# Weighted sums of both halves of a block at its end, products two in the first half and one or none in the second, and two more buffers for the chunks of the mean

## The chip, the cores and the metric

The kernel runs on one core of a Trainium2 chip, in float32 throughout. A core has five engines that run their own queues in order: TensorE (PE; its weight loads are listed apart as PEld), VectorE (DVE), ScalarE (ACT), GpSimd (POOL) and SyncE (SP, which here only issues DMA). Matmul results go to eight banks of PSUM, 2 KB per partition each. The metric is the device time of one execution in microseconds (us), lower is better. The profile is of one execution.

## The reference

Two layers of a Perceiver: 256 query rows of 512 features (x) look at a context of 25088 rows (ctx). Each step adds its result to x after a layer norm.

```
x += x_norm @ W1.T + mean(ctx, rows) @ W2.T + b           # layer 0: the context only through its mean
x += banded self-attention, 16 heads of 32, window 128
x += mixture of 16 experts (4 chosen) + a shared one
Q = x_norm @ Wq + bq;  K = ctx @ Wk + bk;  V = ctx @ Wv + bv     # layer 1: cross-attention
scores[i, j, h] = Q[i, h] . K[j, h] / sqrt(32)
attn = softmax(scores, axis = i)                           # over the 256 queries, for each context row
x += (sum_j attn[i, j, h] V[j, h]) @ Wo + bo
x += windowed self-attention;  x += mixture of 8 experts (2 chosen), layer norm
```

The softmax runs over the queries, so each context row can be finished by itself: its maximum and its sum come from its own 256 scores per head.

## The kernel before

The context is cut into 49 chunks of 512 rows. Chunks 0 to 8 (NPRE) get their keys and values early, and these are stored to DRAM; the other 40 ("late" chunks) get them inside the cross-attention stage.

**Products.** Keys and values of a chunk are 512x512x512 matmuls done by a scheme with seven products of half-size matrices in place of eight (`seven`, line 392). One product is four matmuls of 128x128 by 128x256 (each shows as two records in the profile, so eight records at L401) into one PSUM bank, and is then added on VectorE to one quarter of the result (L423), or to two quarters in the case of one of the seven (S1). GpSimd makes the differences of the chunk that the scheme needs (L387) and one bias addition (L427). A chunk has 14 products.

**PSUM.** `ring` (line 62) is a queue of six banks: `take` gets the first, `give` puts one back at the end. Two more banks (`ac`) hold the sums of the attention. A taken bank is not checked for use; the framework makes its next writer wait for the last reader.

**The start.** From line 491 on: chunks 0 to 6 are loaded into tiles "ck" of the pool `early` (two buffers), and their products run on TensorE. Beside them all other chunks are loaded once for the mean (`load_sum`, L447), each into a tile "ct" of the pool `ctp` (three buffers), and summed by ScalarE (L443). SP issues all these loads in order, eight of the mean's to one ck. At the end `early` is closed; the weights of the first layer, l0x_w (2 MB, L530), the matmuls with them (L544, first with the normalised x, then with the mean), and the self-attention with its weights l0a_wqkv (L550) follow.

**The cross-attention stage** goes over 49 chunks of 4 sub-chunks of 128 context rows: 196 blocks. A block has two halves (`qp`), eight heads each. A half is:

- scores (L740): eight matmuls, four at a time in row groups of 32, into four banks (`scores`). Then for each bank r its maximum over the queries on VectorE (L749), and two exponentials on ScalarE (L754) with their sums. Banks 0 and 1 are given back inside `scores`, banks 2 and 3 after it.
- products of the next late chunk, drawn from the generator `stream` by `fill`. In the kernel before they are drawn in groups of 1, 2, 1, 2, 1 products (seven in five groups), about one group in each half, by a plan that has due times for each chunk. A group of one is drawn in front of bank 3's maximum (`between`), so that its addition stands ahead of that maximum in VectorE's queue; a group of two comes after the scores' work.
- weighted sums (`attend`, L767): eight matmuls, four at a time in column groups of 32. Their weights are the values divided by the sums (`scaled`, on GpSimd, L781, after a reciprocal on VectorE, L775), so a block's weighted sums come after the scores of the following block. The list `waiting` puts one half's weighted sums at the end of each half.

`queue <<` keeps instructions of the stage in the order in which they are written. Exponentials go to four buffers "e", one per half.

Of the kernel before, what the change touches and what calls it, by code (L numbers as in the profile page):

```python
# [9 lines left out]
F32 = mybir.dt.float32  # L10
# [5 lines left out]
P = 128  # L16
# [3 lines left out]
DC = D // P  # L20
# [3 lines left out]
JC = 512  # L24
SUB = JC // P
NPRE = 9
LN_EPS = 1e-5
SCALE = 1.0 / math.sqrt(HD)
# [4 lines left out]
C_L0A_BQ, C_L0A_BK, C_L1X_BQ, C_L1X_BK, C_L1A_BQ, C_L1A_BK = range(6)  # L33
# [4 lines left out]
def perceiver_kernel(  # L38
# [29 lines left out]
    def give(home):  # L68
        ring.append(home)

    def ps_mm(shape=None):
        tile, home = take("mm", shape)
        give(home)
        return tile
# [8 lines left out]
    ctp = ctp_scope.enter_context(tc.tile_pool(name="ctp", bufs=3, side="right"))  # L83
# [6 lines left out]
    early = early_scope.enter_context(tc.tile_pool(name="early", bufs=2, side="right"))  # L90
# [72 lines left out]
    def norm_T(roll=0, fill=None, untransposed=None):  # L163

        xT = work.tile([P, DC, NT], F32, tag="xT", name="xT", bufs=1)
        for t in range(T):
            mean, rs = norm_stats(x[:, t, :])
            xn = work.tile([P, D], F32, tag="xn", name="xn")
            nc.vector.tensor_scalar(xn, x[:, t, :], mean, rs, ALU.subtract, ALU.mult)
            if untransposed is not None:  # L170
                untransposed.append(xn)
            if t == 0 and fill:
                fill(2)
            tp = ps_mm([P, DC, P])
            for dc in range(DC):
                queue << nc.tensor.transpose(tp[:, dc, :], xn[:, dc * P : (dc + 1) * P], ident)
            at = (t * P - roll) % NT
            first = min(P, NT - at)
            nc.vector.tensor_copy(xT[:, :, at : at + first], tp[:, :, :first])
            if first < P:  # L180
                nc.vector.tensor_copy(xT[:, :, : P - first], tp[:, :, first:])
        return xT
# [7 lines left out]
    def feature_major(res, w, xT, col, scale=None):  # L190

        for fc in range(DC):
            ps = ps_mm([P, NT])
            for dc in range(DC):
                queue << nc.tensor.matmul(
                    ps, w[:, dc, fc * P : (fc + 1) * P], xT[:, dc, :],
                    start=dc == 0, stop=dc == DC - 1,
                )
            b = cols[:, col, fc : fc + 1]
            if scale is None:  # L200
                nc.vector.tensor_scalar(res[:, fc, :], ps, b, None, ALU.add)
            else:
                nc.vector.tensor_scalar(res[:, fc, :], ps, b, scale, ALU.add, ALU.mult)
# [239 lines left out]
            nc.scalar.activation(junk, ct[:, dc, :], AF.Identity, accum_out=csum[:, dc, c : c + 1])  # L443

    def load_sum(c):
        ct = ctp.tile([P, DC, JC], F32, tag="ct", name="ct")
        nc.sync.dma_start(out=ct, in_=ctx_d[c])  # L447
        chunk_sum(c, ct)

# [48 lines left out]
    for c in range(FIRST):  # L498
        units = early_chunk(c)
        n = min(8, len(rest)) if c + 1 < FIRST else len(rest)  # L500
# [115 lines left out]
    pending = None  # L616
    for e in range(NE0 + 1):
# [18 lines left out]
        pending = (e, hT, wt)  # L636
# [4 lines left out]
    with tc.tile_pool(name="xa", bufs=2) as xa:  # L641
        e_like = xa.tile([P, H // 2, NT], F32, tag="e", name="wq", bufs=4)
        wq = e_like.rearrange("p a b -> p (a b)").rearrange("p (c d) -> p c d", c=DC)
# [4 lines left out]
        late = list(range(NPRE, NCH))  # L648
        sequence, n = [], 0
# [58 lines left out]
                        yield step  # L708

        stream = projections()  # L710

        groups, done = (1, 2, 1, 2, 1), 0
        total = 2 * len(groups) * len(late)

        def fill(upto):
            nonlocal done
            while done < min(upto, total):
                for _ in range(groups[done % len(groups)]):
                    next(stream)
                done += 1  # L720

        fill(5)
        qT = xa.tile([P, DC, NT], F32, name="qT", bufs=1)
        feature_major(qT, wq, norm_T(fill=lambda n: fill(7)), C_L1X_BQ, SCALE)
        acc = [ps_ac([P, 2, NT]) for _ in range(2)]

        def restore(c):
# [7 lines left out]
        def scores(c, s, qp, e, nm, sm, between, finally_):  # L735
            sc, homes_of = zip(*(take("sc", [P, 2, NT]) for _ in range(4)))
            for i in range(2):
                for r in range(4):
                    part = slice(32 * r, 32 * r + 32)
                    queue << nc.tensor.matmul(  # L740
                        sc[r][:, i, :],
                        kTs[c][part, 2 * qp + i, s * P : (s + 1) * P],
                        qT[part, 2 * qp + i, :],
                        start=True, stop=True,
                    )
            for r in range(4):
                if r == 3:
                    between()
                queue << nc.vector.tensor_reduce(  # L749
                    nm[:, 2 * qp : 2 * qp + 2, r], sc[r], AX.X, ALU.max, negate=True  # L750
                )
                for i in range(2):
                    q = 2 * qp + i
                    queue << nc.scalar.activation(  # L754
                        e[:, 4 * i + r, :], sc[r][:, i, :], AF.Exp,
                        bias=nm[:, q, r : r + 1], accum_out=sm[:, q, r : r + 1],
                    )
                if r < 2:
                    give(homes_of[r])
            finally_()  # L760
            return homes_of[2:]

        def attend(first, last, qp, es, v):
            for i in range(2):
                for r in range(4):
                    h = 4 * (2 * qp + i) + r
                    queue << nc.tensor.matmul(  # L767
                        acc[qp][32 * r : 32 * r + 32, i, :],
                        v[:, h * HD : (h + 1) * HD], es[qp][:, 4 * i + r, :],
                        start=first and i == 0, stop=last, skip_group_check=True,  # L770
                    )
# [19 lines left out]
        due = [(0, done), (halves_of, total)]  # L791
        for at, c in enumerate(sequence):
            if c >= NPRE:
                k = 2 * len(groups) * (c - NPRE)
                due += [(2 * SUB * at, k + len(groups)), (2 * SUB * at + 2, k + 2 * len(groups))]
        plan, at = [done], due[0]
        while at[0] < halves_of:
            slope, to = max(((d[1] - at[1]) / (d[0] - at[0]), d) for d in due if d[0] > at[0])
            plan += [math.ceil(at[1] + slope * k) for k in range(1, to[0] - at[0] + 1)]
            at = to  # L800
        pending, n, waiting = None, 0, []
        restore(sequence[0])
        for c, following in zip(sequence, [*sequence[1:], None]):
            for s in range(SUB):
                if s == SUB - 1 and following is not None and following < NPRE:
                    restore(following)
                assert c < NPRE or ("k", c) in made
                nm = small.tile([P, Q, 4], F32, tag="nm", name="nm")
                sm = small.tile([P, Q, 4], F32, tag="sm", name="sm")
                es = []  # L810
                for qp in range(2):
                    e = xa.tile([P, H // 2, NT], F32, tag="e", name="e", bufs=4)
                    es.append(e)

                    def finally_():
                        if qp == 0 and pending is not None:
                            pc, ps, psm = pending[2]
                            pending[1][1] = scaled(pc, ps, inverse(psm))

                    def between():  # L820
                        if done < plan[n + 1] and groups[done % len(groups)] == 1:
                            fill(done + 1)

                    last = scores(c, s, qp, e, nm, sm, between, finally_)
                    n += 1
                    fill(min(plan[n], done + 1))
                    give(last[0])
                    fill(plan[n])
                    give(last[1])
                    assert qp == 0 or c < NPRE or ("v", c) in made  # L830

                    while waiting:
                        attend(*waiting.pop())
                    if pending is not None:
                        waiting.append((*pending[0], qp, *pending[1]))
                pending = ((n == 2, n == halves_of), [es, None], [c, s, sm])
            finished(c)
        pc, ps, psm = pending[2]
        pending[1][1] = scaled(pc, ps, inverse(psm))
        attend(*waiting.pop())  # L840
        for qp in range(2):
            attend(*pending[0], qp, *pending[1])

# [96 lines left out]
    upto = mini([P, NE1], "upto")  # L940
# [261 lines left out]
```

## Time and profile before

| | |
|---|---|
| median of 3 runs | 2849.3 us (2839.3 to 2852.96) |
| profiled execution | 2845.46 us, span 2843.7 us, mean granted TensorE clock 0.983 |
| TensorE busy | 2765.5 us (97%) |
| VectorE busy | 1727.7 us (61%) |
| ScalarE busy | 1712.9 us (60%) |
| stage of scores, 618 to 2467 us: TensorE, VectorE, ScalarE busy | 1849.7, 1412.6, 1470.7 us of 1851 |
| 8 to 165 us: TensorE busy, DMA share, rate | 146.3 of 157 us, 0.99, 393 GB/s |

The span is what lies between the first and the last instruction. A busy share is an average; matmuls are pipelined and the ends of their records are modelled, so durations of a group are best read from start to start. An entry in square brackets behind a row is the engine's idle time before it and what ended it.

### The profile page before, as it was taken

Reading aid. Unit: us, or ns where it says so; the run is one execution under the profiler, and the core shown is the slowest. Engines: PE = TensorE matmul, PEld = TensorE weight load, DVE = VectorE, ACT = ScalarE, POOL = GpSimd, SP = SyncE. Lnnn points to the kernel's source line nnn. Section 1 sums busy time; section 2 is a strip of 40 time slices with the busy share of each in tenths; the row PEclk is TensorE's granted clock in tenths of the full one; section 3 lists DMA queues with packets and bytes.
Section 4 is the critical chain, followed back from the end, with each engine's and each line's share of the span. In section 5 each row is a group of like instructions: output and inputs, shape, how many; then the busy total and the mean of one; then the engine's idle time right before and its main releaser. Section 6 shows DMA issues by size and latency. Waiting matters only on the chain. (4 is left out here: it accounts for less than half of the span.)

```text
span 2843.7 us, 56628 instructions
## 1 busy us (share of the span) xinstructions
PE 2765.5 (97%) x21236; PEld 1945.7 (68%) x21236; DVE 1727.7 (61%) x3065; ACT 1712.9 (60%) x7025; POOL 577.5 (20%) x532
## 2 busy tenths in 40 slices
PE   8998999999999999999999999999999999878998
PEld 7876777776666666666666666666666666556775
DVE  4345511147777777777777777777777777642101
ACT  6732100027778778778878878878888888621111
POOL 4221100012222323222222222222223222100000
PEclk9998999999999999999999999999999999978999
DMA  9971443410101010100101000101000101107774
GB/s 358 405 303 71 174 166 145 155 60 31 46 16 46 16 46 31 46 31 31 46 16 46 31 31 31 46 26 36 31 31 31 46 16 46 44 2 270 264 270 152
DMA packets 38099, 262.32 MB, mean 92 GB/s; under 512 B 4984, under 2 KB 8104, under 8 KB 10432
## 3 DMA queue, kind: packets, MB, share of 16 engines
q1 hardware_dynamic: 34640, 237.32, 22.2%
q0 software_dynamic: 3184, 21.33, 1.8%
q8 instruction: 173, 2.83, 0.4%
q14 instruction: 102, 0.84, 0.1%
HBM read 239.23 MB, written 19.40 MB: 91 GB/s over the span
## 5 line engine op out<-in xcount | busy, mean ns | idle before, releaser
L754 ACT ACTIVATE e<-ps_sc,nm 128x256 f32<-128x256 f32 x3136 | 1437.8, 484 | 376.7 <-DVE nm L749 376.4
L749 DVE TENSOR_REDUCE nm<-ps_sc 128x2 f32<-128x512 f32 x1568 | 994.6, 685 | 358.8 <-PE ps_sc L740 358.8
L754 ACT ACTIVATION_READ_ACCUMULATOR e<-ps_sc,nm 128x1 f32 x3136 | 676.9, 216 | 0.0
L767 PE MATMUL ps_ac<-e,vs 128*32 128x256 f32 x6272 | 421.6, 387 | 4.1 <-POOL vs L781 4.1
L401 PE MATMUL ps_kv<-ts,wq 128*128 128x256 f32 x1568 | 388.9, 392 | 9.1 <-DVE wq L365 6.5
L401 PE MATMUL ps_kv<-wq,ts 128*128 128x256 f32 x1568 | 386.8, 391 | 0.0
L781 POOL TENSOR_TENSOR vs<-v,rc 128x512 f32<-128x512 f32 x160 | 167.9, 1049 | 1015.7 <-DVE rc L775 1015.7
L401 PEld LDWEIGHTS ps_kv<-ts,wq 128*128 128x128 f32 x1568 | 287.0, 191 | 95.4 <-issue 26.7
L401 PEld LDWEIGHTS ps_kv<-wq,ts 128*128 128x128 f32 x1568 | 286.0, 190 | 84.7 <-issue 26.5
L740 PE MATMUL ps_sc<-qT,kT 32*128 32x256 f32 x4096 | 303.1, 401 | 1.3 <-ACT e L754 1.1
L767 PEld LDWEIGHTS ps_ac<-e,vs 128*32 128x32 f32 x6272 | 164.4, 109 | 202.6 <-issue 114.6
L423 DVE TENSOR_TENSOR v<-v,ps_kv 128x512 f32<-128x512 f32 x343 | 227.5, 676 | 102.1 <-PE ps_kv L401 57.6
L740 PEld LDWEIGHTS ps_sc<-qT,kT 32*128 32x128 f32 x4096 | 191.1, 184 | 116.0 <-ACT e L754 105.9
L401 PE MATMUL ps_kv<-wq,ct 128*128 128x256 f32 x1008 | 244.7, 386 | 0.0
L401 PE MATMUL ps_kv<-ct,wq 128*128 128x256 f32 x1008 | 242.4, 383 | 0.0
L423 DVE TENSOR_TENSOR kT<-kT,ps_kv 128x512 f32<-128x512 f32 x280 | 186.9, 680 | 64.6 <-PE ps_kv L401 54.2
L401 PEld LDWEIGHTS ps_kv<-wq,ct 128*128 128x128 f32 x1008 | 189.9, 192 | 38.3 <-ACT e L754 12.9
L401 PEld LDWEIGHTS ps_kv<-ct,wq 128*128 128x128 f32 x1008 | 188.1, 190 | 38.1 <-ACT e L754 12.6
L627 PE MATMUL ps_mm<-xT,we 128*128 128x256 f32 x816 | 178.8, 379 | 0.0
L627 PEld LDWEIGHTS ps_mm<-xT,we 128*128 128x128 f32 x816 | 155.0, 190 | 27.4 <-issue 7.2
L1091 ACT ACTIVATE hT<-ps_mm,b 128x128 f32<-128x128 f32 x128 | 36.6, 368 | 211.7 <-PE ps_mm L1085 158.2
L632 ACT ACTIVATE sg<-ps_mm 128x256 f32<-128x256 f32 x51 | 19.6, 385 | 229.4 <-PE ps_mm L627 229.4
(218 smaller groups left out, 2265.9 us busy)
## 6 DMA issues: line engine op xcount, KB each, us to landing
ct<-in_ctx_dram SPq DMA_DIRECT2D x84, 1024.0 KB, 6.4
we<-in_l1e_dram SPq DMA_DIRECT2D x64, 1024.0 KB, 6.8
we<-in_l0e_dram SPq DMA_DIRECT2D x17, 2304.0 KB, 8.6
kv<-kT POOLq DMA_DIRECT2D x9, 1024.0 KB, 9.9
kv<-v POOLq DMA_DIRECT2D x9, 1024.0 KB, 9.7
vp<-kv SPq DMA_DIRECT2D x9, 1024.0 KB, 5.0
kTp<-kv SPq DMA_DIRECT2D x8, 1024.0 KB, 4.8
ck<-in_ctx_dram SPq DMA_DIRECT2D x6, 1024.0 KB, 9.5
```

The source lines that it names most:

```text
L401: queue << nc.tensor.matmul(ps[:, m, :], fixed[:, d, m * P : (m + 1) * P], moving[:, d, :], start=d == 0, stop=d == 1,)
L423: queue << nc.vector.tensor_tensor(to, old, ps, ALU.subtract if a == W_A22 else ALU.add)
L627: queue << nc.tensor.matmul(gu[:, k, :], wk[:, dc, ic * P : (ic + 1) * P], xT[:, dc, :], start=dc == 0, stop=dc == DC - 1,)
L632: nc.scalar.activation(sg, gu[:, 0, :], AF.Silu)
L740: queue << nc.tensor.matmul(sc[r][:, i, :], kTs[c][part, 2 * qp + i, s * P : (s + 1) * P], qT[part, 2 * qp + i, :], start=True, stop=True,)
L749: queue << nc.vector.tensor_reduce(nm[:, 2 * qp : 2 * qp + 2, r], sc[r], AX.X, ALU.max, negate=True)
L754: queue << nc.scalar.activation(e[:, 4 * i + r, :], sc[r][:, i, :], AF.Exp, bias=nm[:, q, r : r + 1], accum_out=sm[:, q, r : r + 1],)
L767: queue << nc.tensor.matmul(acc[qp][32 * r : 32 * r + 32, i, :], v[:, h * HD : (h + 1) * HD], es[qp][:, 4 * i + r, :], start=first and i = ...
L781: queue << nc.gpsimd.tensor_mul(vs.rearrange("p (h d) -> p h d", h=H), vs_of[c, s].rearrange("p (h d) -> p h d", h=H), rc.unsqueeze(2).to_ ...
L1091: nc.scalar.activation(hT[:, fc, :], ps[:, fc, :], AF.Gelu, bias=b1[:, hf * FC + fc : hf * FC + fc + 1])
```

## The change

In the stage, the groups and the list `waiting` are gone. The plan is drawn up for whole blocks (`course`, in steps of two halves), and a block's products are split: up to two in the first half, the rest in the second. A product of the second half, if it is one, is drawn in front of bank 3's maximum (`between`); those of the first are drawn after the scores' work, one ahead of giving back bank 2 and one ahead of bank 3. The weighted sums of both halves of the block before are issued at the end of the second half. At the start, the mean's chunks go to two more buffers, tiles "cs" of the pool `early`, two chunks in five.

```diff
     def load_sum(c):
-        ct = ctp.tile([P, DC, JC], F32, tag="ct", name="ct")
+
+        if c % 5 in (1, 3):
+            ct = early.tile([P, DC, JC], F32, tag="cs", name="cs")
+        else:
+            ct = ctp.tile([P, DC, JC], F32, tag="ct", name="ct")
         nc.sync.dma_start(out=ct, in_=ctx_d[c])
         chunk_sum(c, ct)
...
-        groups, done = (1, 2, 1, 2, 1), 0
-        total = 2 * len(groups) * len(late)
+        total, done = 14 * len(late), 0
 
         def fill(upto):
             nonlocal done
             while done < min(upto, total):
-                for _ in range(groups[done % len(groups)]):
-                    next(stream)
+                next(stream)
                 done += 1
 
-        fill(5)
+        fill(7)
         qT = xa.tile([P, DC, NT], F32, name="qT", bufs=1)
-        feature_major(qT, wq, norm_T(fill=lambda n: fill(7)), C_L1X_BQ, SCALE)
+        feature_major(qT, wq, norm_T(fill=lambda n: fill(10)), C_L1X_BQ, SCALE)
...
             if c >= NPRE:
-                k = 2 * len(groups) * (c - NPRE)
-                due += [(2 * SUB * at, k + len(groups)), (2 * SUB * at + 2, k + 2 * len(groups))]
-        plan, at = [done], due[0]
+                k = 14 * (c - NPRE)
+                due += [(2 * SUB * at, k + 7), (2 * SUB * at + 2, k + 14)]
+        course, at = [done], due[0]
         while at[0] < halves_of:
             slope, to = max(((d[1] - at[1]) / (d[0] - at[0]), d) for d in due if d[0] > at[0])
-            plan += [math.ceil(at[1] + slope * k) for k in range(1, to[0] - at[0] + 1)]
+            course += [math.ceil(at[1] + slope * k) for k in range(2, to[0] - at[0] + 1, 2)]
             at = to
-        pending, n, waiting = None, 0, []
+        plan = []
+        for a, b in zip(course, course[1:]):
+            plan += [min(2, b - a), max(0, b - a - 2)]
+        pending, n = None, 0
...
                     def between():
-                        if done < plan[n + 1] and groups[done % len(groups)] == 1:
+                        if plan[n] == 1:
                             fill(done + 1)
 
+                    upto = done + plan[n]
                     last = scores(c, s, qp, e, nm, sm, between, finally_)
                     n += 1
-                    fill(min(plan[n], done + 1))
-                    give(last[0])
-                    fill(plan[n])
-                    give(last[1])
+                    for home in last:
+                        fill(min(upto, done + 1))
+                        give(home)
+                    fill(upto)
                     assert qp == 0 or c < NPRE or ("v", c) in made
 
-                    while waiting:
-                        attend(*waiting.pop())
-                    if pending is not None:
-                        waiting.append((*pending[0], qp, *pending[1]))
+                if pending is not None:
+                    for qp in range(2):
+                        attend(*pending[0], qp, *pending[1])
                 pending = ((n == 2, n == halves_of), [es, None], [c, s, sm])
             finished(c)
         pc, ps, psm = pending[2]
         pending[1][1] = scaled(pc, ps, inverse(psm))
-        attend(*waiting.pop())
         for qp in range(2):
             attend(*pending[0], qp, *pending[1])
```

## The prediction

> **What bounds the kernel now.** I read the table of busy times and the 40 slices first, then TensorE's waits, then its timeline inside the long cross-attention stage.
>
> ```profile
> span 2843.7 us, 56628 instructions
> PE 2765.5 (97%) x21236; PEld 1945.7 (68%) x21236; DVE 1727.7 (61%) x3065; ACT 1712.9 (60%) x7025; POOL 577.5 (20%) x532
> ...
> PE ps_sc L740 <- ACT e L754: 1.1, 5, 0.3
> ```
>
> TensorE (PE) is busy for 97%, and in the slices of the stage of scores (618 to 2467 us, 1846 us from its first scores to its last) for 90% or more throughout: here PE's own time counts. The last line, from TensorE's waits, says that scores waited for ScalarE's exponentials 1.1 us in all: a bank of PSUM was nearly always free in time. How near that is, the timeline shows (start, length, group of instructions):
>
> ```profile
> 1202.23 1.15 PE L740 MATMUL ps_sc<-qT,kT 32*128 32x256 f32 x16
> 1203.31 1.99 PE L401 MATMUL ps_kv<-ts,wq 128*128 128x256 f32 x8
> 1205.14 1.89 PE L401 MATMUL ps_kv<-ct,wq 128*128 128x256 f32 x8
> 1206.96 1.07 PE L767 MATMUL ps_ac<-e,vs 128*32 128x256 f32 x16
> 1207.96 1.15 PE L740 MATMUL ps_sc<-qT,kT 32*128 32x256 f32 x16
> 1209.03 1.99 PE L401 MATMUL ps_kv<-ts,wq 128*128 128x256 f32 x8
> 1210.96 1.07 PE L767 MATMUL ps_ac<-e,vs 128*32 128x256 f32 x16
> 1211.96 1.15 PE L740 MATMUL ps_sc<-qT,kT 32*128 32x256 f32 x16
> ```
>
> From start to start: scores (S) 1.07, one product (P) 1.93, two 3.65, weighted sums (A) 1.00. A half with one product takes 4.00 (1207.96 to 1211.96), one with two 5.73; two halves with three products 9.73, with two 8.00.
>
> The exponentials behind the scores of 1207.96 set when banks come free:
>
> ```profile
> 1209.91 0.47 ACT L754 ACTIVATE e<-ps_sc,nm 128x256 f32<-128x256 f32 x1 [1.97 <-DVE nm L749]
> ...
> 1211.63 0.21 ACT L754 ACTIVATION_READ_ACCUMULATOR e<-ps_sc,nm 128x1 f32 x1
> ```
>
> The first starts 1.95 after the scores (a maximum on VectorE lies between). Bank 1 of the scores (of 0 to 3) is read out at 1211.84, 3.88 after the scores began; bank 2 one pair of exponentials later (pairs start at 1209.91, 1210.82, 1211.72 in the same view), at 1212.75, 4.79 after. A half that lasts 4.00 and whose successor asks for bank 1 has 0.12 to spare.
>
> **The change, part by part.** *(1) Weighted sums of both halves at the block's end.* The built order of the changed kernel is S P P S P A A for a block of three products, S P P S A A for one of two. Working the plan out gives 164 blocks of three, 29 of two, and three empty ones at the end (where before also has six empty halves). The matmuls are the same; what goes is one group A between other groups. At the stage's end 32 records of A that follow each other last 1.93 where 16 last 1.07, so a second A costs 0.86, not 1.00. Three products: S P P 4.72, then S P A A 1.07+1.93+1.86 = 4.86, sum 9.58, or 0.15 under 9.73. Two: 4.72 + 1.07+1.86 = 7.65, or 0.35 under 8.00 (a switch into and out of products goes too). PE's own gain: 164 x 0.15 + 29 x 0.35 = 35 us.
>
> The Trainium skill agrees with the sign (TensorEngine Tiling (Array Packing), Key Properties: changing the tiling mode drains the engine), and by that rule alone the stage would end 35 us sooner. The same page speaks against it under PSUM Bottleneck: tiling speeds up the matmuls, not the emptying of PSUM, and the copy out can become the limit. It has no price; the rows above have one, and they decide, as follows.
>
> *(2) What the removed sums covered.* A ring of six banks serves S (four) and P (one each). Following the ring: after S P P the next scores ask for banks 0 and 1 of this half's scores, the first product's bank, and bank 2 of the scores. Bank 2 comes at 4.79 + 0.05 (the way of the semaphore, from restarts of PE at the stage's end); the fourth score matmul would start at 4.72 + 0.02. So 0.08 to 0.1 late, in about 140 blocks (after an empty second half the exponentials start earlier): 11 us. Before, the sums of 1.00 stood there.
>
> In the 29 blocks of two the second half is S A A, 2.93 of PE work, and the next scores ask last for its bank 1, free at 3.93. PE runs its queue in order, and behind that matmul stand the rest of the scores, the products and the sums of the half, so about 0.9 is lost each time: 26 us. Before shows this state at its end, six halves without a product (ScalarE's lines left out):
>
> ```profile
> 2457.37 1.32 PE L740 MATMUL ps_sc<-qT,kT 32*128 32x256 f32 x6
> 2458.91 1.12 PE L740 MATMUL ps_sc<-qT,kT 32*128 32x256 f32 x10 [0.22 <-ACT e L754]
> 2460.05 1.07 PE L767 MATMUL ps_ac<-e,vs 128*32 128x256 f32 x16
> 2461.06 1.29 PE L740 MATMUL ps_sc<-qT,kT 32*128 32x256 f32 x6
> ```
>
> The scores begin, stop after 6 of 16 records until ScalarE frees a bank, and the half takes 3.69 where PE needs 2.07.
>
> One product in seven is added twice on VectorE (0.60 each). As first product of a half its bank is free only at 3.57 (four maxima) + 0.24 (reciprocal) + 0.60 + 0.69 = 5.10 and the next scores want it at 4.74; as second product it is free at 6.2 and the second half's product, which now takes that same bank, wants it at 5.88. That is some 0.27 more in about 45 blocks: 12 us. In before such a half shows 4.04 for 4.00.
>
> Sum of the stage: -35 + 11 + 26 + 12 = +14. Bounds: -35 with no wait at all; +38 if each of the 140 waits is 0.25 and not 0.08. I take +14, whose largest term has a precedent in the trace.
>
> *(3) Two more buffers for the mean's chunks.* Between 20 and 190 us DMA moves 400 to 425 GB/s with the engines full, apart from 0.82 in 20 to 30 and 0.91 in 50 to 60: at most 2.7 us to win, and the order of bytes ahead of each chunk that PE waits for (2.2 us at 139.06, 2.7 at 168.30) is unchanged. I take -1.5 (0 to -2.7). SP and POOL issue the same transfers, SP's mean chunks up to two earlier.
>
> But the buffers lie in the pool that is closed just before the weights of the first layer are loaded, and in the built order that load (L530 before, L534 after) now carries waits on the seventh chunk's last use by PE, on ScalarE and on POOL; before it had none. It also slips behind three context loads on SP, and l0a_wqkv and the next context chunk stand behind it there.
>
> ```profile
> 166.22 0.42 SPq L530 DMA_DIRECT2D l0x_w<-in_l0x_w_dram  x1
> ```
>
> ```profile
> 192.97 1.89 PE L401 MATMUL ps_kv<-wq,ck 128*128 128x256 f32 x8
> ...
> 197.96 7.13 PE L544 MATMUL ps_mm<-l0x_w,xT 128*128 128x512 f32 x16 [0.51 <-DVE xT L179]
> ...
> 223.19 7.11 PE L195 MATMUL ps_mm<-xT,l0a_wqkv 128*128 128x256 f32 x24 [3.45 <-DMA l0a_wqkv<-in_l0a_wqkv_dram]
> ```
>
> The last product that reads ck is the one of 192.97, done at 194.9, so 2 MB can be asked for only then. 3 MB took 11.0 us on an idle queue (l0a_wqkv, issued at 212.04), 1 MB 5.0 (vp): 2 MB is 8.0. It lands at 202.9, the matmuls of 197.96 slip 5.0 us, and all behind them with it (l0a_wqkv, asked for after they end, slips as much, so its own wait stays). Bounds: 3.3 (6.4 us, the median of a context chunk) to 9 (12.2, its own time before). A gap of that length also costs clock: after the 3.45 us wait before 223.19 the granted clock was 0.63 and 0.52 until 227 (1.7 us lost), after the one before 168.30 it was 0.5 to 0.7 until 176 (3.3 lost). I take 2 more. Together +5.5.
>
> Sum against the profiled execution (2845.5 us, of which the span is 2843.7): +14 + 5.5 = +19.5, so 2865. The median of the runs is 3.8 above the profiled one: 2868; I write 2867.
>
> **The rivals.** *About the same, 2854 (chance 0.28).* The waits are half as dear: after a late bank VectorE's maxima come 0.4 sooner relative to the restart, so waits don't add, and the better-filled DMA pays for the late weights. For it: such restarts in the tail catch up. Against: in-order PE. Stage +5, start 0.
> *Faster, 2820 (chance 0.06).* Only PE's switches count, -35, with the start at +5.5. It decides once the three waits cost under 15 us instead of 49; the 3.88 of bank 1 against 2.93 makes that unlikely.
> *Much slower, 2896 (chance 0.14).* VectorE becomes late: two additions between the maxima of adjoining halves delay the exponentials, each first half waits 0.25 (stage +38), and the late weights cost their upper end (+9.5). Against: by the rows VectorE is done 1 us before the next half's first maximum.
> *No effect of the order* is excluded: the build shows it.
>
> **How the numbers follow.** The likeliest case has 0.52 and spans 2858 to 2878. The 80% range reaches into its neighbours: 2850 to 2885. About 0.5% (14 us) is what a measurement can tell from no change: faster below 2835, slower above 2863.5. Most of the likeliest case (0.48) and all of the worst one are slower, 0.62; the flat case and the rest are the same, 0.32; 0.06 faster.
>
> **What would show it.** In TensorE's timeline of the changed kernel: blocks of 9.6 to 9.7 with A as 32 records; waits of scores for exponentials of some tens of us in place of 1.1, most of it after halves S A A, with scores broken up as above; a wait of some 5 us for l0x_w near 198. The stage from first to last scores 1860 rather than 1846. Wrong if A A costs 2.00, if blocks of two take under 8.0, or if the load of l0x_w is not late.

## The result, and the profile after

The changed kernel takes 2866.4 us (median of 6 runs, 2863.64 to 2872.03); the kernel before, beside it, 2847.1 (6 runs, 2838.56 to 2852.96). The ratio is 1.0075, 95% interval 1.0053 to 1.0096: slower, by 19 us. The forecast was 2867. It is right in the sum, and the sum hides two errors that nearly cancel.

The page of the changed kernel, head and busy times:

```profile
span 2862.0 us, 56556 instructions
...
PE 2769.7 (97%) x21236; PEld 1994.4 (70%) x21236; DVE 1715.5 (60%) x3065; ACT 1717.1 (60%) x7025; POOL 577.0 (20%) x532
```

TensorE's waits in the stage of scores (line, what it waited for: us in all, times, longest):

```profile
PE ps_sc L741 <- ACT e L755: 8.6, 38, 1.4
PE ps_kv L401 <- DVE kT L423: 5.2, 17, 0.4
...
PE ps_kv L401 <- DVE v L423: 2.9, 9, 0.4
```

Scores waited 1.1 us for exponentials before, and products for VectorE's additions not at all. That names some 17 us, of which 14 lie ahead of the last six halves, where before has none. The timeline shows more (start, length, group; S is L741, P is L401, A is L768):

```profile
1213.85 1.25 PE L741 MATMUL ps_sc<-qT,kT 32*128 32x256 f32 x16
1215.03 1.99 PE L401 MATMUL ps_kv<-wq,ts 128*128 128x256 f32 x8
1216.95 1.93 PE L768 MATMUL ps_ac<-e,vs 128*32 128x256 f32 x32
1218.82 1.15 PE L741 MATMUL ps_sc<-qT,kT 32*128 32x256 f32 x16
1219.89 1.99 PE L401 MATMUL ps_kv<-wq,ct 128*128 128x256 f32 x8
1221.72 1.89 PE L401 MATMUL ps_kv<-wq,ts 128*128 128x256 f32 x8
1223.54 1.25 PE L741 MATMUL ps_sc<-qT,kT 32*128 32x256 f32 x16
```

The half S P P lasts 4.72 (1218.82 to 1223.54), as worked out, and 32 records of A 1.87. But the scores behind S P P start to start take 1.18 and not 1.07 (1213.85 to 1215.03): 0.11 of wait that no bracket shows; it lies inside the scores' record, which is 1.25 long and not 1.15. A block of three products takes 9.69 to 9.70. A block of two:

```profile
1098.63 1.25 PE L741 MATMUL ps_sc<-qT,kT 32*128 32x256 f32 x16
1099.81 1.93 PE L768 MATMUL ps_ac<-e,vs 128*32 128x256 f32 x32
1101.67 0.71 PE L741 MATMUL ps_sc<-qT,kT 32*128 32x256 f32 x6
1102.57 1.12 PE L741 MATMUL ps_sc<-qT,kT 32*128 32x256 f32 x10 [0.19 <-ACT e L755]
1103.62 1.99 PE L401 MATMUL ps_kv<-ct,wq 128*128 128x256 f32 x8
```

and ScalarE's exponentials for the scores of 1098.63 (the first of eight, and the end of the fourth):

```profile
1100.58 0.47 ACT L755 ACTIVATE e<-ps_sc,nm 128x256 f32<-128x256 f32 x1 [0.97 <-DVE nm L750]
...
1102.30 0.21 ACT L755 ACTIVATION_READ_ACCUMULATOR e<-ps_sc,nm 128x1 f32 x1
```

S A A is over after 3.04; bank 1 is read out at 1102.51, 3.88 after its scores began, and TensorE goes on at 1102.57. The scores take 1.95 from start to start (1101.67 to 1103.62), 0.88 more than their own 1.07; the bracket shows 0.19 of it.

From the first scores to the last record of the last sums the stage took 1857.7 us before (618.6 to 2476.3) and takes 1882.3 now (612.3 to 2494.6): 24.7 more. What follows it is equal. What precedes it is 6.4 shorter. TensorE's waits and DMA at the start, before:

```profile
139.06 1.97 PE L401 MATMUL ps_kv<-ck,wq 128*128 128x256 f32 x8 [2.19 <-DMA ck<-in_ctx_dram]
...
168.30 3.18 PE L401 MATMUL ps_kv<-ck,wq 128*128 128x256 f32 x8 [2.73 <-DMA ck<-in_ctx_dram]
```

and after (the first line is SP's issue of the weights of the first layer):

```profile
185.09 0.33 SPq L534 DMA_DIRECT2D l0x_w<-in_l0x_w_dram  x1
```

```profile
163.97 1.99 PE L401 MATMUL ps_kv<-ts,wq 128*128 128x256 f32 x8 [1.82 <-POOL ts L387]
...
192.74 8.72 PE L548 MATMUL ps_mm<-l0x_w,xT 128*128 128x512 f32 x16 [5.19 <-issue]
...
219.10 15.74 PE L195 MATMUL ps_mm<-xT,l0a_wqkv 128*128 128x256 f32 x64 [2.99 <-DMA l0a_wqkv<-in_l0a_wqkv_dram]
```

The two waits for ck are gone, and with the second the half clock behind it (TensorE reaches its last product of the start 9.9 us sooner than before). Then comes the wait for l0x_w, 5.19 where 5.0 was forecast, and its matmuls run slower, 8.72 for 7.13, at a granted clock of 0.57 from 192 to 196. The gain behind the matmuls with l0x_w is 3.6 (the next product starts at 208.17, before at 211.80), and 6.4 at the first scores; the 2.8 between them lie within what the start varies by itself (below), and their cause is open.

Stretches of the start, before (stretch, its length, busy us and counts of PE, PEld, DVE, ACT, POOL, granted clock, DMA share, GB/s):

```profile
20.00:60.00 40.00, 40.00 (x187) 35.22 (x186) 22.30 (x38) 30.12 (x97) 14.59 (x14) 1.00 0.93 373
60.00:100.00 40.00, 40.00 (x188) 35.20 (x187) 18.20 (x27) 30.92 (x99) 11.51 (x12) 1.00 1.01 403
100.00:130.00 30.00, 29.80 (x138) 25.93 (x137) 12.70 (x19) 22.47 (x73) 8.36 (x8) 1.00 1.01 399
```

and after:

```profile
20.00:60.00 40.00, 40.00 (x187) 35.22 (x186) 21.72 (x37) 33.20 (x107) 14.96 (x15) 1.00 1.01 422
60.00:100.00 40.00, 40.00 (x187) 35.22 (x186) 18.42 (x28) 32.73 (x104) 11.16 (x11) 1.00 1.01 423
100.00:130.00 30.00, 30.00 (x140) 26.41 (x139) 13.37 (x20) 22.93 (x73) 8.34 (x8) 1.00 1.01 423
```

A DMA share of 1.01 stands for 399 to 403 GB/s in the one and for 423 in the other. A full share was no ceiling.

### The profile page after: what moved, and what is told of

It reads as the page before. It is cut to its first block, busy times and chain, and to the rows that moved or that the text cites. A ratio compares the mean times of both kernels' runs of the same rounds, so it can differ in the third digit from the quotient of the medians.

```text
span 2862.0 us, 56556 instructions
## 1 busy us (share of the span) xinstructions
PE 2769.7 (97%) x21236; PEld 1994.4 (70%) x21236; DVE 1715.5 (60%) x3065; ACT 1717.1 (60%) x7025; POOL 577.0 (20%) x532
## 5 line engine op out<-in xcount | busy, mean ns | idle before, releaser
L768 PE MATMUL ps_ac<-e,vs 128*32 128x256 f32 x6272 | 381.9, 384 | 4.1 <-POOL vs L782 4.1
L401 PE MATMUL ps_kv<-ts,wq 128*128 128x256 f32 x1568 | 377.5, 387 | 4.9 <-POOL ts L387 4.9
L401 PE MATMUL ps_kv<-wq,ts 128*128 128x256 f32 x1568 | 378.0, 386 | 0.0
L401 PEld LDWEIGHTS ps_kv<-ts,wq 128*128 128x128 f32 x1568 | 290.9, 190 | 73.3 <-ACT e L755 12.9
L401 PEld LDWEIGHTS ps_kv<-wq,ts 128*128 128x128 f32 x1568 | 289.3, 190 | 69.4 <-DVE v L423 15.3
L741 PE MATMUL ps_sc<-qT,kT 32*128 32x256 f32 x4096 | 326.0, 402 | 6.0 <-ACT e L755 6.0
L768 PEld LDWEIGHTS ps_ac<-e,vs 128*32 128x32 f32 x6272 | 184.5, 110 | 172.2 <-issue 57.1
L741 PEld LDWEIGHTS ps_sc<-qT,kT 32*128 32x128 f32 x4096 | 209.1, 184 | 115.0 <-ACT e L755 67.4
L401 PE MATMUL ps_kv<-ct,wq 128*128 128x256 f32 x1008 | 246.9, 388 | 5.8 <-DVE kT L423 5.2
L401 PE MATMUL ps_kv<-wq,ct 128*128 128x256 f32 x1008 | 247.3, 388 | 2.9 <-DVE v L423 2.9
L401 PEld LDWEIGHTS ps_kv<-ct,wq 128*128 128x128 f32 x1008 | 184.1, 190 | 58.4 <-PE ps_sc L741 12.9
L401 PEld LDWEIGHTS ps_kv<-wq,ct 128*128 128x128 f32 x1008 | 186.4, 191 | 51.0 <-issue 8.0
L741 PE MATMUL ps_sc<-qT,kTp 32*128 32x256 f32 x2176 | 172.9, 402 | 2.6 <-ACT e L755 2.6
```

Source lines behind the costliest of these rows:

```text
L401: queue << nc.tensor.matmul(ps[:, m, :], fixed[:, d, m * P : (m + 1) * P], moving[:, d, :], start=d == 0, stop=d == 1,)
L741: queue << nc.tensor.matmul(sc[r][:, i, :], kTs[c][part, 2 * qp + i, s * P : (s + 1) * P], qT[part, 2 * qp + i, :], start=True, stop=True,)
L768: queue << nc.tensor.matmul(acc[qp][32 * r : 32 * r + 32, i, :], v[:, h * HD : (h + 1) * HD], es[qp][:, 4 * i + r, :], start=first and i = ...
```

## The experiments

First all of them in one table. "First scores" and "stage" (to the last record of the last sums) are from each kernel's profiled execution. The start varies by itself: seven kernels with before's start, itself among them, have their first scores between 617.0 and 621.6. A row without a ratio is a single run, beside 2844.7 for the kernel before (*unsummed* beside 2846.6).

| kernel | us | ratio, 95% interval | first scores | stage |
|---|---|---|---|---|
| before | 2846.6 | | 618.6 | 1857.7 |
| changed | 2866.4 | 1.0075, 1.0053 to 1.0096 | 612.3 | 1882.3 |
| order | 2872.5 | 1.0086, 1.0072 to 1.0099 | 619.7 | 1884.9 |
| buffers | 2841.5 | 0.9981, 0.9973 to 0.9989 | 615.0 | 1858.4 |
| buffers_free | 2836.4 | 0.9969, 0.9958 to 0.9980 | 607.2 | 1858.3 |
| held | 2858.7 | 1.0048, 1.0036 to 1.0060 | 617.0 | 1870.5 |
| before_nosum | 2842.4 | | 620.9 | 1854.6 |
| order_nosum | 2845.4 | | 619.0 | 1857.8 |
| order_oneuse | 2864.5 | | 619.3 | 1871.2 |
| one_one | 2886.1 | | 621.6 | 1895.0 |
| four_free | 2836.8 | 0.9962, 0.9949 to 0.9975 | 610.5 | 1858.3 |
| shared_sum | 2857.8 | 1.0040, 1.0025 to 1.0056 | 628.9 | 1858.2 |
| unsummed | 2837.3 | | 609.5 | 1857.5 |

### The two parts apart

*order*: the changed kernel without its new buffers.

```diff
     def load_sum(c):
-        if c % 5 in (1, 3):
-            ct = early.tile([P, DC, JC], F32, tag="cs", name="cs")
-        else:
-            ct = ctp.tile([P, DC, JC], F32, tag="ct", name="ct")
+        ct = ctp.tile([P, DC, JC], F32, tag="ct", name="ct")
```

> The changed order of the stage of scores alone, with before's three buffers for the mean's chunks. Theory: the stage loses 24.7 us in the changed kernel's trace (1873.3 against 1848.7 from the first scores to the start of the last sums) whatever happens before it, so the time is before + 25, about 2872, and the start (first scores near 618.6) is as before. Rival (the prediction's sums): stage +14, about 2861. Second rival: the stage is long because it begins after another start, then less than +10.

*buffers*: the kernel before with only that edit of `load_sum`, the other way round.

> The five buffers alone, with before's stage of scores. Theory: the start wins what the changed kernel's trace shows, first scores 6.4 us sooner, so about 2841; the load of l0x_w is asked for near 185 and TensorE waits some 5 us for it. Rival (the prediction's step: DMA was full already, so only the late weights count): first scores 5.5 us later, about 2853.

Measured: 2872.5 and 2841.5, as the theory has it; both forecasts of the prediction's sums (2861, 2853) are missed. The stage of *order* is 27.2 longer than before: all its halves but the last six together 22.8 (23.3 in the changed kernel), the last six, which have no product, 4.4 (1.4); that tail differs from kernel to kernel. The two parts add: +25.9 and -5.2 is +20.7, against +19.3 for the change. So the order costs, and the buffers win. The first scores of *buffers* come 3.6 us sooner, where 6.4 was expected. TensorE's timeline of *buffers* repeats that of the changed kernel, the wait for l0x_w with it:

```profile
192.80 8.62 PE L548 MATMUL ps_mm<-l0x_w,xT 128*128 128x512 f32 x16 [5.24 <-issue]
...
219.77 12.48 PE L195 MATMUL ps_mm<-xT,l0a_wqkv 128*128 128x256 f32 x49 [3.71 <-DMA l0a_wqkv<-in_l0a_wqkv_dram]
```

### What the order's loss consists of

All kernels of this part have before's three buffers.

*held*: no half without a product; a block of two has its products as 1 and 1, and one group of sums waits for its first half.

```diff
-            plan += [min(2, b - a), max(0, b - a - 2)]
+            plan += [(b - a + 1) // 2, (b - a) // 2]
...
                     fill(upto)
+                    while held:
+                        attend(*held.pop())
...
                 if pending is not None:
-                    for qp in range(2):
-                        attend(*pending[0], qp, *pending[1])
+                    attend(*pending[0], 0, *pending[1])
+                    held.append((*pending[0], 1, *pending[1]))
+                    if n == halves_of or sum(plan[n : n + 2]) > 2:
+                        attend(*held.pop())
```

> Three buffers; the sums of a block are held so that no half is without a product or short of sums: products 2 and 1, or 1 and 1 in a block of two; ahead of a block of two one group of sums waits for that block's first half. Orders S P P S P A | S P A S P A A for a pair of three and two, S P P S P A A elsewhere. Theory: the pair takes 8.73 + 8.97 = 17.70 and not 18.34 us (9.70 for three products, 4.73 + 3.04 + 0.87 of waiting for two), so 29 x 0.64 = 18.6 us of the order's 24.7 go, about 2853. Rival: the loss sits in the halves S P P and S P A A themselves, then the stage stays within 5 us of the changed order's, about 2870.

Measured: the stage is 14.4 shorter than in *order*, 12.8 over before and not 6; 2858.7 where 2853 was expected. The direction is the theory's, and the rival (nothing gained) falls. Most of the missing 7 us stands in its 59 halves S P A, 4.16 in the mean where 4.00 was expected: most of those behind S P P take 4.10 (the bank-2 wait of 0.1 is in them too), and 17 take 4.35 to 4.49.

*one_one*: the same even split, but with both sums at the block's end as in *order*.

```diff
-            plan += [min(2, b - a), max(0, b - a - 2)]
+            plan += [(b - a + 1) // 2, (b - a) // 2]
```

> The changed order (three buffers), but a block of two products has one in each half: S P S P A A in place of S P P S A A; no half is without a product. Theory: what counts is that a half must not end before 3.93 us, when bank 1 is read out. S P of 3.00 is as short as S A A of 2.93, so the wait of 0.9 only moves: the two halves take 3.00 + 0.93 + 4.97 = 8.9, and the stage is some 5 us longer than the changed order's 1884.9. Rival: a half without a product is what costs (one more switch in a row, no cover for VectorE), then the 29 x 0.87 = 25 us go, and the stage is about 1860.

Measured: stage 10.1 longer than in *order*. Expected was 5, the rival -25. A half without a product is not what costs; a half that is too short is (TensorE's timeline of *one_one*; in the kernels without the new buffers S is L737 and A L764):

```profile
1105.15 1.15 PE L737 MATMUL ps_sc<-qT,kT 32*128 32x256 f32 x16
1106.22 1.99 PE L401 MATMUL ps_kv<-ct,wq 128*128 128x256 f32 x8
1108.15 0.72 PE L737 MATMUL ps_sc<-qT,kT 32*128 32x256 f32 x4
1109.08 1.13 PE L737 MATMUL ps_sc<-qT,kT 32*128 32x256 f32 x12 [0.22 <-ACT e L751]
```

S P is done after 3.00, the next scores stop at once, and go on at 1109.08, 3.93 after the scores of 1105.15 began: within 0.01 of the 3.94 of the empty half (1098.63 to 1102.57). The two halves take 8.84 in the mean (3.00 + 5.84), against 8.65 for S P P, S A A and the wait behind it: 29 x 0.19 = 5.5. The rest of the 10.1 lies in other halves and in the tail.

*before_nosum* and *order_nosum*: the exponentials of the stage without their sums, so that banks of scores come free sooner.

```diff
-                        bias=nm[:, q, r : r + 1], accum_out=sm[:, q, r : r + 1],
+                        bias=nm[:, q, r : r + 1],
...
-                sm = small.tile([P, Q, 4], F32, tag="sm", name="sm")
...
+        sm = xa.tile([P, Q, 4], F32, name="sm1", bufs=1)
+        nc.vector.memset(sm, 1.0)
```

> The kernel before with the exponentials in the stage of scores not summed (the sums of the weights are left out, a tile of ones stands in for them), so that ScalarE hands the banks of scores back sooner. Theory: before, banks are in time already, so the stage (first scores to the end of the last sums, 1857.7 us) stays within 3 us, and halves stay 5.73 and 4.00; only the last empty halves shorten.

> The changed order (three buffers) with the same sums left out. Theory: TensorE waits in it for banks that ScalarE holds; without them the order shows its own worth on TensorE, 35 us less than before, of which the products added twice still cost some 13: stage 20 to 35 us under that of the kernel before with the sums left out, S P P 4.72, S P A A 4.86 (5.2 where a product is added twice), S A A 2.93 with no wait of 0.87 after it. Rival: the loss lies on TensorE itself (switches, the later sums): the stage is still some 25 us over.

Measured: in the kernel before the last six halves get 6.4 us shorter and all others 3.4 longer (the 42 halves behind a product added twice go from 4.04 to 4.11), together 3.0 us. *order* gives 27.1, 19.3 of it ahead of the last six halves. The order's loss shrinks from 27.2 to 3.2, ahead of the last six halves from 22.8 to 0.2: it hangs on how long exponentials hold the banks. That it does not turn into a gain of 20 misses the expectation, and the halves tell why. S P P is 4.73 and S P A A 4.86, TensorE's own times: the bank-2 wait is gone. But the half behind S A A is still 5.34 (5.60 with the sums), as TensorE's timeline of *order_nosum* shows:

```profile
1101.71 1.93 PE L764 MATMUL ps_ac<-e,vs 128*32 128x256 f32 x32
1103.57 1.76 PE L737 MATMUL ps_sc<-qT,kT 32*128 32x256 f32 x16
1105.26 1.99 PE L401 MATMUL ps_kv<-ct,wq 128*128 128x256 f32 x8
```

ScalarE's view of it:

```profile
1102.58 3.03 ACT L751 ACTIVATE e<-ps_sc,nm 128x256 f32<-128x256 f32 x8 [1.63 <-DVE nm L746]
```

An exponential without its sum still takes 3.03 / 8 = 0.38 (0.45 with it), and the first starts 1.95 after the scores as before, so bank 1 comes at 1.95 + 4 x 0.38 = 3.47, half a microsecond behind the end of S A A. And 44 halves with a product added twice take 5.3, since VectorE's additions are not touched. 28 x 0.61 + 44 x 0.43 = 36 us of waits stand against what TensorE gains, and the two nearly cancel. In *order* the waits are 57 us, so leaving the sums out took away about 20 and not all.

*order_oneuse*: the second addition left out.

```diff
-            (W_S1, ts[:, 0], ((c22, c21), (c12, c12))),
+            (W_S1, ts[:, 0], ((c22, c21),)),
```

> The changed order (three buffers), with the second addition of the product that is added twice left out (so one quarter of keys and values lacks a term). Theory: 45 halves wait 0.24 to 0.33 for that product's bank, so the stage is some 13 us shorter than with it (1884.9 to about 1872), and S P A A of 5.2 and 5.3 become 4.86 to 4.97. Rival: those halves are long for another reason (the block's place, the bank of the scores), then the stage stays within 3 us.

Measured: stage 13.7 shorter (1871.2), and the halves S P A A of 5.2 to 5.3 become 4.86 to 4.97, all but two. The 28 waits of TensorE for VectorE's kT, v and kTp in the changed kernel (17 + 9 + 2) fit the halves of 5.30 that follow a product added twice as second of its half. TensorE's timeline of the changed kernel shows one:

```profile
1039.88 1.15 PE L741 MATMUL ps_sc<-qT,kTp 32*128 32x256 f32 x16
1041.42 1.97 PE L401 MATMUL ps_kv<-wq,ct 128*128 128x256 f32 x8 [0.39 <-DVE v L423]
1043.31 1.93 PE L768 MATMUL ps_ac<-e,vs 128*32 128x256 f32 x32
```

### Why more buffers help

*buffers_free*: the kernel before with two more buffers that do not stand in the way of l0x_w.

```diff
     early_scope = ExitStack()
+    cs_scope = ExitStack()
     early = early_scope.enter_context(tc.tile_pool(name="early", bufs=2, side="right"))
+    csp = cs_scope.enter_context(tc.tile_pool(name="csp", bufs=2, side="right"))
...
     def load_sum(c):
-        ct = ctp.tile([P, DC, JC], F32, tag="ct", name="ct")
+        if c % 5 in (1, 3) and c < 40:
+            ct = csp.tile([P, DC, JC], F32, tag="cs", name="cs")
+        else:
+            ct = ctp.tile([P, DC, JC], F32, tag="ct", name="ct")
...
+    cs_scope.close()
     early_scope.close()
```

> Five buffers with before's stage, but the two new ones lie at the free end of the memory and only chunks below 40 use them, so that the load of l0x_w waits for nothing. Theory: the buffers' whole gain stays: 6.4 us as in the changed kernel, plus the 5.2 us wait and the 1.6 to 3.6 us of slower clock after it: first scores 13 us sooner than before, about 2834. Rival: the 2 MB of l0x_w, asked for some 20 us sooner, take the DMA from the chunks that TensorE waits for, and the waits for ck and ts come back: first scores only 4 to 7 us sooner, about 2841.

Measured: 2836.4, ratio 0.9969 (0.9958 to 0.9980), faster than both kernels. The load of l0x_w is asked for at 158.22 and its matmuls wait 0.55 (5.24 in *buffers*); they take 7.11 again and not 8.62. First scores 11.4 us sooner than before (13 was expected, 4 to 7 by the rival). So the late load cost what the prediction said, and what the buffers win ahead of it is about 10 us, not 1.5.

*four_free*: the same with one more buffer and not two (`c % 4 == 1`, `bufs=1`).

> One more buffer for the mean's chunks and not two (every fourth chunk below 40, at the free end of the memory, the load of l0x_w waits for nothing), before's stage. Theory: three buffers leave DMA too little in flight while ScalarE sums a chunk; a fourth covers most of it: 415 to 422 GB/s between 20 and 130 us, first scores 9 to 12 us sooner than before, about 2836. Rival: the rate grows by equal steps with each buffer: 408 GB/s, first scores 5 to 6 us sooner, about 2841.

Measured: 2836.8; 412, 421 and 422 GB/s in the three stretches, first scores 8.1 us sooner (9 to 12 expected, 5 to 6 by the rival). One buffer does nearly all.

*unsummed*: three buffers, but chunks from the eighth on are loaded and not summed (the mean is taken over the first seven).

```diff
     def chunk_sum(c, ct):
...
-        for dc in range(DC):
-            junk = ...
+        if c < FIRST:
+            for dc in range(DC):
+                junk = ...
```

> Three buffers, before's stage; the mean's chunks are loaded but not summed (the mean is taken over the first seven chunks alone), so a buffer is free as soon as it has landed. Theory (a buffer is held for the 2.45 us of ScalarE's sums): 420 GB/s and more between 20 and 130 us with three buffers, first scores 9 to 12 us sooner. Rival (the number of loads in flight alone): within 5 of before's 400 GB/s, first scores as before.

Measured, in the same stretches:

```profile
20.00:60.00 40.00, 40.00 (x187) 35.20 (x187) 21.90 (x37) 5.60 (x18) 14.64 (x14) 1.00 1.01 409
60.00:100.00 40.00, 40.00 (x187) 35.22 (x186) 18.21 (x27) 2.56 (x8) 11.39 (x12) 1.00 1.01 414
100.00:130.00 30.00, 30.00 (x141) 26.41 (x140) 13.36 (x20) 2.56 (x8) 8.32 (x8) 1.00 1.01 420
```

Three buffers do it too, if nothing holds them after they have landed; first scores at 609.5, 9.1 sooner. The rate falls a little short of the expected 420 at first, but the rival (the number of buffers alone) falls. Nor is it ScalarE's reading of the chunks that slows the loads: *four_free* keeps all of it and has 421 to 422.

*shared_sum*: three buffers, two of the four sums of each chunk on VectorE.

```diff
         for dc in range(DC):
+            if c >= FIRST and dc >= 2:
+                nc.vector.tensor_reduce(csum[:, dc, c : c + 1], ct[:, dc, :], AX.X, ALU.add)
+                continue
```

> Three buffers, before's stage, but of the four sums of each of the mean's chunks two are taken by VectorE, so that a buffer is held some 1.2 us after its landing and not 2.45. Theory: the rate is set by how long a buffer is held; it rises from 400 to 410 to 422 GB/s, and with it the waits for ck go, first scores 6 to 11 us sooner, about 2839. Rival: only the number of loads in flight counts: 400 GB/s as before, about 2847. What could spoil it: VectorE takes its queue in order, and a sum that waits for its chunk holds the additions that TensorE's banks wait for.

Measured: 2857.8, slower, by what the expectation named as its spoiler. VectorE, by its waits between 20 and 160 us, stood still for chunks that had not landed,

```profile
DVE csum L443 <- DMA ct<-in_ctx_dram: 42.9, 17, 6.9
```

TensorE waited 15 us for its additions, and the loads ran at 381 to 385 GB/s. It says nothing on how long a buffer may be held.

## Why the prediction was right, and where it was not

**The time.** 2867 against 2866.4, but stage +14 and start +5.5 were in truth +24.7 and -6.4. The sum, 18.3, agrees with 19.5 by luck. (2865 and 3.8 are 2868.8 and not 2868; that changes nothing.)

**(1) TensorE's own gain: right.** 35 us were forecast. All halves but the last six take 1852.0 us in the changed kernel; less the 57 us of waits below they come to 1795, against 1828.7 before: 34. A A takes 1.86 to 1.87 and S P P 4.73, as worked out. No kernel had all waits removed, so the 34 are worked out, from the measured sums and from TensorE's own times for each kind of half.

**(2) The waits: the right three, sized too small.** Against TensorE's own 4.73, 4.86 and 2.93:

| wait | forecast | measured |
|---|---|---|
| scores behind S P P, for bank 2 | 0.08 x 140 = 11 | 0.11 in most: 15 in S P A A, 3 in S A A |
| scores behind S A A, for bank 1 | 0.9 x 29 = 26 | 0.88 x 28 = 25 |
| the product added twice | 0.27 x 45 = 12 | 14 (*order_oneuse*) |
| sum | 49 | 57 |

The step that failed in size is "0.08 to 0.1 late, in about 140 blocks": it is about 0.11, and the S A A halves have it too. With 34 for 35, and 1.4 from the tail, that is the way from +14 to +24.7. The bank-1 time of 3.88, read from one half of the kernel before, is the same to the hundredth in the half of the changed kernel shown above, and it set the 3.93 of *one_one*. The flat rival, by which the waits are half as dear and do not add, is out: the waits came to 57 us and not to half of 49, and the double addition, forecast at 12, gave back 13.7 when it was left out. The reading of the Trainium skill's PSUM Bottleneck (TensorEngine Tiling (Array Packing)), that emptying PSUM can become the limit, was the one to follow: about 20 of the 57 us of waits went with the sums of the exponentials.

**(3) The start: wrong in sign.** The step that failed: "Between 20 and 190 us DMA moves 400 to 425 GB/s with the engines full", so "at most 2.7 us to win" and "I take -1.5". The share was taken for a limit. Before's own profile spoke against both readings, in the view of stretches of 10 us:

```profile
100.00:110.00 10.00, 10.00 (x48) 8.81 (x47) 2.75 (x4) 7.62 (x27) 0.00 (x0) 1.00 1.01 425
110.00:120.00 10.00, 9.80 (x46) 8.32 (x45) 5.52 (x9) 9.98 (x33) 8.36 (x8) 1.00 1.01 355
...
140.00:150.00 10.00, 8.17 (x38) 6.89 (x37) 5.92 (x9) 9.03 (x30) 7.42 (x8) 1.00 1.00 355
```

The rate fell to 355 GB/s twice, not to 400 at the least, and the same share of 1.01 stood beside 355 and beside 425. With a fourth buffer, or with three that ScalarE does not hold for its 2.45 us, the same queue moved 409 to 422 GB/s; the chunks that TensorE waits for landed earlier though the order of bytes ahead of them was the same, and of the two waits for ck (2.2 and 2.7 us) the first went and at most 1.1 us of the second was left, and the half clock went: 10 us in the changed kernel. The other term stood: l0x_w late by 5.2 (5.0 forecast), 1.6 of clock (2 forecast), with *buffers_free* as the counter-test. So -10 + 7 = -3; at the first scores it was -3.6 in *buffers* and -6.4 in the changed kernel, which differ by what the start varies by itself.

**What would show it.** Blocks of 9.6 to 9.7: seen. The wait of some 5 us for l0x_w: seen, at 193 and not 198. Scores waiting some tens of us: in truth yes, in the view of waits no: it names 8.6. The rest is inside the scores' records, start to start 1.18 and 1.95 where 1.07 is TensorE's. From the first scores to the last the stage takes 1869.5, where 1860 was forecast and before has 1846.0.

## What to carry to other kernels

Where TensorE runs in order round a ring of PSUM banks, the half between two uses of a bank has a least length, here 3.93 us where bank 1 is asked for and 4.84 where bank 2 is. Merging groups of matmuls to save switches makes some halves shorter than that, and here the saving (34 us) came back as waits (57 us). Read that length from the first consumer's start and its pace before moving work, and measure halves from start to start: the view of waits showed 14 of the 57.

For streams through a few buffers, a full DMA share does not say that the rate can't rise. Ask how long a buffer is held after landing, try one more, and see that the new buffer does not lie where the next load must go: that alone was 5 us of time here (2841.5 against 2836.4).

## What the runs showed of the hardware that was not expected

- The mean busy share of the DMA engines was 1.01 at 399 to 403 GB/s and at 421 to 423 GB/s, so it was no measure of the rate; what it counts is not shown.
- Leaving the sum out of an exponential (128x256) shortened ScalarE's pace from 0.45 to 0.38 us only, though the read of the accumulator shows as 0.21.
- A gap of 2.7 us in TensorE's work at 165 to 168 was followed by half-speed matmuls (3.18 and 3.77 us for groups of 1.97), at a granted clock of 0.50 from 169 to 174; a gap of 1.82 at 162 to 164 in the changed kernel was not (1.99). The length alone does not decide: of two gaps of 2.39 and 2.38 us in TensorE's timeline of *order*, only the second was (granted clock 1.00 from 140 to 146, 0.50 from 170 to 174).

```profile
140.08 1.97 PE L401 MATMUL ps_kv<-ck,wq 128*128 128x256 f32 x8 [2.39 <-DMA ck<-in_ctx_dram]
...
168.97 2.94 PE L401 MATMUL ps_kv<-ck,wq 128*128 128x256 f32 x8 [2.38 <-DMA ck<-in_ctx_dram]
```
